# Attention with a conditioning vector: exponentials one by one, the sums of x earlier in VectorE's order, K's halves as Q's, and a rearranged front

## The chip, the core and the metric

The kernel runs on one core of a Trainium2 chip. The core has five engines with instruction queues of their own: TensorE (PE in the profile; its weight loads are shown as PEld), VectorE (DVE), ScalarE (ACT), GpSimd (POOL) and SyncE (SP, which here only issues DMAs). They work side by side and wait for one another through semaphores; each engine works through its own queue in order. Matrix products land in PSUM, which the kernel uses as eight banks of 128 x 512 float32 values; everything else lies in SBUF.

The metric is the device time of one execution in microseconds (us), lower is better. The kernel before takes 751.83 us (median of 3 runs, 751.81 to 753.56).

## The reference

The input `x` is 8 sequences of 512 rows of 512 features, `cond_1024` one vector of 512 for each sequence. All is float32. Cut to what matters:

```python
def reference(x, cond_1024, Wq, bq, Wk, bk, Wv, bv):      # 16 heads of 32
    tokens = cond_1024[:, None, :]
    Q = split_heads(x @ Wq.T + bq)
    K = split_heads(x @ Wk.T + bk)
    V = split_heads(x @ Wv.T + bv)
    cQ = Q + split_heads(tokens @ Wq.T + bq)
    cK = K + split_heads(tokens @ Wk.T + bk)
    scores = einsum('bhqd,bhkd->bhqk', cQ, cK) / sqrt(32)
    out = einsum('bhqk,bhkd->bhqd', softmax(scores), V)
    return x + merge_heads(out)
```

## The kernel before

**Units of work.** Four heads (128 features) of one sequence make one unit t; there are 8 x 4 = 32 of them, and b, r = divmod(t, 4) are its sequence and its group of heads. For each t the scores are computed twice: once with the queries in the rows (`row_scores`, L490), for the row maximum (`row_max_of`, L499, on VectorE, two banks at a time) and for the denominators (`denominators`, L527, four activations on ScalarE that only leave their sums), and once with the keys in the rows (`exponentials`, L569 and L572), where L569 first puts the negative maximum into the bank and L572 adds the scores. ScalarE takes the exponentials out of these banks (L584, L586). They stay in SBUF, and an iteration later `weighted` multiplies them with V (`times_v`, L591).

**The loop.** An iteration t of the main loop (t = 0 to 28) has four steps. Each step opens with `exponentials(t, k)` and `row_max(t+1, ...)`, and then holds one more piece of work on TensorE:

- step 0: a part of the projection Q of the next sequence (`project_pair("q")`);
- step 1: `weighted(t-1)`, and for r = 0 and 1 a half of `combine_x(b+1)`;
- step 2: a part of K's projection;
- step 3: a part of V's projection, and the transposing of the next maxima (`transpose_max`, L553).

At t = 0 the steps hold what is left of the first sequence's projections instead.

**The projections** of all but the first heads are done with seven half-size products in place of eight, per 2 x 2 blocks. `combine_x` makes the sums and differences of blocks of x that this takes (tile `xc`; L321, L322 for half 0, L324, L325 for half 1; each 128 x 512), `combine_w` those of the weights. `first_products` does products 1, 6, the half kc = 0 of product 2, and 7; `other_products` does 4, 5, the rest of product 2, and 3. In steps, Q's and K's first products run at odd r and their other products at even r, V's the other way round: the step for Q and K is one iteration behind (`qk_of`). K differs from Q in how product 2 is divided: in `first_products` only the first 128 of its 256 columns, in `other_products` the second part of these and both parts of the remaining 128 columns, as six matmuls of 128 columns (two per part, each float32 matmul being two instructions in the trace). A copy on GpSimd (L438) stands for the part that the first half leaves out.

**`weighted`** (t-1, in step 1) multiplies on TensorE into one bank, takes the reciprocal of the denominators (L637, VectorE), turns the bank in 32 x 32 blocks into SBUF (L639, VectorE), and leaves the multiplication and the addition of x to GpSimd (L640, L641) before four DMAs write the output.

**Order.** The instruction order on TensorE, ScalarE, VectorE and GpSimd is the program's own, written by hand. PSUM's banks are given out by the table `TURNS`: each step has a row of eight bank numbers; `banks(0..3)` are for the exponentials and, once these are taken out, for the step's further work; `banks(4..7)` are for the row scores. `advance()` goes to the next row; rows 0 to 7 repeat in the loop, 8 to 12 serve the end, 13 to 17 the first denominators before the loop. `banks(i, 2)` gives two banks as one operand with a stride: banks 3 and 7 make one operand of the first step's maximum in row 17.

**The front.** The four row blocks of the first sequence are loaded through SP's and ScalarE's queues, two each, then the conditioning vectors and two biases through ScalarE's (`cond_sb`, L199 to L201) and the weights through SP's. TensorE transposes x (`transpose_x`, L299), then the conditioning (L718), then the weights (`transpose_w`, L254), and projects Q and K of the first heads (L338). A one-column exponential, `table` (L241), makes ScalarE load its function table; it stands behind all constants in the program, behind all the loads on ScalarE's queue.

Of the kernel before, what the change touches and what calls it, by code (L numbers as in the profile page):

```python
# [9 lines left out]
F32 = mybir.dt.float32  # L10
# [7 lines left out]
def kernel(  # L18
# [38 lines left out]
    nc = tc.nc  # L57
# [46 lines left out]
    ]  # L104
    turn = [0]

    def banks(i, n=1):

        j = TURNS[turn[0]][i]
        if n == 1:  # L110
            return psum[:, j, :]
        k = TURNS[turn[0]][i + 1]
        return psum[:, j : k + 1 : k - j, :]
# [13 lines left out]
    def load_x(n, queue=nc.sync):  # L127

        if n < B * NS:
            xs[n] = xp.tile([P, D], F32, tag="x", name=f"x_{n}")  # L130
            queue.dma_start(xs[n], x[n // NS, n % NS * P : (n % NS + 1) * P, :])
# [62 lines left out]
    load_x(1, nc.scalar)  # L194
    load_x(2)
    load_x(3, nc.scalar)

    cond_sb = const.tile([B + 2, D], F32, tag="cond", name="cond_sb")
    nc.scalar.dma_start(cond_sb[:B, :], cond)  # L199
# [16 lines left out]

    ident = const.tile([P, P], F32, tag="ident", name="ident")
    make_identity(nc, ident)
    onesb = const.tile([P, P], BF16, tag="onesb", name="onesb")
    nc.vector.memset(onesb, 1.0)  # L220
    ones = const.tile([P, P], F32, tag="ones", name="ones")
    nc.vector.memset(ones, 1.0)
    split = []
    for i in range(2):
        m = const.tile([P, NS, HG, HD], BF16, tag=f"split{i}", name=f"split{i}")
# [11 lines left out]
    nc.vector.memset(condT, 0.0)  # L237
    identb = const.tile([P, P], BF16, tag="identb", name="identb")
    nc.vector.tensor_copy(identb, ident)
    table = const.tile([P, 1], F32, tag="table", name="table")  # L240
    nc.scalar.activation(table, ones[:, :1], AF.Exp)  # L241
    xc = const.tile([P, 4, 2, HS], F32, tag="xc", name="xc")
    vs = [const.tile([P, NS, D], F32, tag=f"v{i}", name=f"v{i}") for i in range(2)]

# [46 lines left out]
    def transpose_x(n, pt, leaves=nc.vector.tensor_copy):  # L291

        b, sc = divmod(n, NS)
        if b >= B:
            return
        if sc == 0:
            xT[b] = xtp.tile([P, NC, S], F32, tag="xT", name=f"xT_{b}")
        for cc in range(NC):
            nc.tensor.transpose(  # L299
                pt[:, cc * P : (cc + 1) * P], xs[n][:, cc * P : (cc + 1) * P], ident  # L300
            )
        leaves(xT[b][:, :, sc * P : (sc + 1) * P], pt.rearrange("p (c s) -> p c s", c=NC))
        load_block(n + NC)
# [74 lines left out]
    def block_of_x(b, i, kc, at):  # L378
        f = MADE_OF[i - 1][1]
        if isinstance(f, int):  # L380
            return xc[:, f, kc, at]
        off = HS * (f == "22")
        return xT[b][:, kc + 2 * (f != "11"), at.start + off : at.stop + off]

    def product(n, b, u, i, pt, kcs=(0, 1), cols=None):


        for kc in kcs:
            w = block_of_w(n, i, u, kc)
            if n == "v":  # L390
                xb = block_of_x(b, i, kc, slice(u * P, (u + 1) * P))
                nc.tensor.matmul(pt, xb, w, start=(kc == kcs[0]), stop=(kc == kcs[-1]))  # L392
            else:
                xb = block_of_x(b, i, kc, cols or slice(0, HS))
                nc.tensor.matmul(pt, w, xb, start=(kc == kcs[0]), stop=(kc == kcs[-1]))  # L395

    def twice(a):
# [22 lines left out]
    def first_products(n, b, u, dens, small, at, first=0):  # L420

        one_, two_ = banks(first), banks(at)
        c1, c12, c2, c22 = parts_of(n, b, u)
        m1 = c2[:, 0, :]
        product(n, b, u, 1, one_[:, :HS])
        nc.scalar.copy(m1, one_[:, :HS])
        dens()
        product(n, b, u, 6, two_[:, :HS])  # L430
        small()
        w = P if n == "k" else HS
        product(n, b, u, 2, two_[:, HS : HS + w], (0,), slice(0, w))
        product(n, b, u, 7, one_[:, HS:])
        nc.vector.tensor_tensor(c12, two_[:, :HS], m1, ALU.add)
        nc.vector.tensor_tensor(c1[:, 0, :w], two_[:, HS : HS + w], m1[:, :w], ALU.add)
        if w < HS:
            nc.gpsimd.tensor_copy(c1[:, 0, w:], m1[:, w:])  # L438
        plus(n, b, u, 1, c22, one_[:, HS:], c12)

    def other_products(n, b, u, dens, small, at):

        dens()
        one_, two_ = banks(at[0]), banks(at[1])
        product(n, b, u, 4, one_[:, :HS])
        product(n, b, u, 5, one_[:, HS:])
        small()
        if n == "k":
            product(n, b, u, 2, two_[:, :P], (1,), slice(0, P))
            product(n, b, u, 2, two_[:, P:HS], (1, 0), slice(P, HS))  # L450
        else:
            product(n, b, u, 2, two_[:, :HS], (1,))
        product(n, b, u, 3, two_[:, HS:])
        c1, c12, c2, c22 = parts_of(n, b, u)
        nc.vector.tensor_tensor(c12, one_[:, HS:], c12, ALU.add)
        nc.vector.tensor_tensor(c2, halves(one_), twice(c22), ALU.add)
        plus(n, b, u, 0, c1, halves(two_), c1)
        if n != "v":
            for g in range(2):
                qkT[n, b * G + u * 2 + g] = pair_of(b * G + u * 2, n)[:, g, :]  # L460
# [103 lines left out]
    def exponentials(t, kc, at=None):  # L564

        bank = [psum[:, i, :] for i in at] if at else [banks(i) for i in range(HG)]
        for j in range(HG):
            r = slice(j * HD, j * HD + 3)
            nc.tensor.matmul(bank[j], onesb[r, :], maxT[t][r, :], start=True, stop=False)  # L569
        for j in range(HG):  # L570
            r = slice(j * HD, (j + 1) * HD)
            nc.tensor.matmul(  # L572
                bank[j],
                qkT["k", t][r, kc * P : (kc + 1) * P],
                qkT["q", t][r, :],
                start=False,
                stop=True,
            )
        for pr in range(NP):
            e = ep.tile([P, 2, S], F32, tag="e", name=f"e_{t}_{kc}_{pr}")  # L580
            es[t, kc, pr] = e
            if pr == 0 or at:
                for i in range(2):
                    nc.scalar.activation(e[:, i, :], bank[pr * 2 + i], AF.Exp)  # L584
            else:
                nc.scalar.activation(e, banks(2, 2), AF.Exp)  # L586

    def times_v(t, kc, pt, chunks=range(NS)):
        b, g = divmod(t, G)
# [22 lines left out]
        oT[t] = op.tile([P, S], F32, tag="oT", name=f"oT_{t}")  # L612
        nc.vector.tensor_copy(oT[t], pt)

    def weighted(t, pt, pd):


        apart = op.tile([P, HG, NS, NS], F32, tag="apart", name=f"apart_{t}")
        nc.gpsimd.tensor_tensor(
            apart,  # L620
            sums[t].rearrange("p c h o -> p h c o").broadcast_to([P, HG, NS, NS]),
            which.unsqueeze(1).unsqueeze(1).broadcast_to([P, HG, NS, NS]),
            ALU.mult,
        )
        for kc in range(NS):
            times_v(t, kc, pt)
            if kc == 0:
                for h in range(HG):
                    nc.tensor.matmul(
                        pd[h * BL : (h + 1) * BL, : NB],  # L630
                        modulo,
                        apart[:, h].rearrange("p c a -> p (c a)"),
                        start=True,
                        stop=True,
                    )
        rec = op.tile([P, NB, 1], F32, tag="recs", name=f"recs_{t}")
        nc.vector.reciprocal(rec, pd[:, :NB].unsqueeze(2))  # L637
        y = op.tile([P, NB, BL], F32, tag="res", name=f"res_{t}")
        nc.vector.transpose(y.rearrange("p f e -> p (f e)"), pt)  # L639
        nc.gpsimd.tensor_tensor(y, y, rec.broadcast_to([P, NB, BL]), ALU.mult)  # L640
        nc.gpsimd.tensor_tensor(y, y, xr.pop(t), ALU.add)  # L641
        b, g = divmod(t, G)
        for h in range(HG):
            nc.sync.dma_start(spread(out[b], g * P + h * BL), y[h * BL : (h + 1) * BL])
# [67 lines left out]

    for c in range(NS):
        transpose_x(c, bank((3, 7, 0, 1)[c]), nc.scalar.copy if c % 2 else nc.vector.tensor_copy)
    pc = bank(5)
    BB = B + 2
    for cc in range(NC):
# [5 lines left out]
    bias2 = const.tile([P, 2, NC], F32, tag="bias2", name="bias2")  # L723
    nc.vector.tensor_scalar(bias2[:, 0, :], pcv[:, :, B], 2.0 * SCALE, None, ALU.mult)
    nc.vector.tensor_scalar(bias2[:, 1, :], pcv[:, :, B + 1], 2.0, None, ALU.mult)
    for half in range(2):
        combine_x(0, half, nc.gpsimd)
    transpose_w("q", 0, bank(6), 1)
    transpose_w("k", 0, bank(3), 0)
    transpose_w("q", 1, bank(7), 1)  # L730
    pq, pk = bank(4), bank(2)
    for cc in range(NC):
        project_qk_part(0, "q", cc, pq)
# [36 lines left out]
    advance()  # L770
    row_max(0, 3)
    split_max(0)
    first_products("v", 0, 0, lambda: denominators(0, 3), nothing, 2, 0)
    turn_x(NC)
    advance()
    row_max(1, 0)
    transpose_max(0, banks(3), nc.scalar.copy)
    other_products("v", 0, 0, lambda: denominators(1, 0), nothing, (0, 2))
    turn_x(NC + 1)
    load_residual(0)  # L780
# [27 lines left out]
    for t in range(T - 3):  # L808
# [16 lines left out]
        dens = lambda: denominators(t + 1, 2)  # L825
        if t:
            dens()
            weighted(t - 1, banks(0), banks(1))
        else:
            first_products("v", 0, 1, dens, nothing, 1)  # L830
        if r < 2:
            combine_x(b + 1, r)
        advance()

        exponentials(t, 2)
# [166 lines left out]
```

## Time and profile before

| | us |
|---|---|
| median of the runs | 751.83 |
| the profiled execution, its own time | 751.59 |
| its span, from first to last instruction | 749.8 |
| granted TensorE clock, mean | 1.000 |
| TensorE busy (matmuls) | 736.8 (98%) |
| ScalarE busy | 621.6 (83%) |
| VectorE busy | 529.4 (71%) |
| GpSimd busy | 178.6 (24%) |

| group | count | mean ns |
|---|---|---|
| L527 denominators, 128 x 512, ScalarE | 496 | 686 |
| L527 reading their sums | 496 | 204 |
| L584 exponentials, 128 x 512, ScalarE | 270 | 596 |
| L586 exponentials, 128 x 1024, ScalarE | 121 | 1032 |
| L428 copy of the first product, 128 x 256, ScalarE | 46 | 372 |
| L499 row maximum of two banks, VectorE | 256 | 1218 |
| L639 turning of the output, VectorE | 28 | 717 |
| L321, L324 first sum of a half, VectorE | 7, 7 | 654, 650 |
| L322, L325 second sum of a half, VectorE | 7, 7 | 1318, 1536 |
| L640, L641 multiply and add, GpSimd | 28, 28 | 1212, 1425 |
| L395 K's 128-column matmuls of product 2 | 120 | 274 |
| L241 table load, ScalarE | 1 | 1283 |

How to read it: matmuls are pipelined, so that the busy time of TensorE includes overlaps and small waits; 98% doesn't mean that it runs at its peak. The mean of an instruction is the time from its start to its end, and on ScalarE and VectorE the next one can start before that end. What one more instruction costs is read from the distance between starts, and only where the engine is not waiting. What a wait costs is read from the step in which it lies: the starts of the L569 matmuls mark the steps, and the main loop's iterations repeat them very evenly.

### The profile page before, as it was taken

The page shows a single profiled execution, that of the slowest core. Times are in us where ns is not written, and L with a number is a line of the kernel's source. Part 1 is how long each engine was busy: PE and PEld are TensorE (multiplying, and loading weights), DVE is VectorE, ACT ScalarE, POOL GpSimd, SP SyncE. Part 2 cuts the span into 40 slices and gives each one's busy share as a digit, 9 for nine tenths or more (in the row PEclk, how much of TensorE's full clock was granted, in tenths as well). Part 3 has the DMA queues.
Part 4 walks back from the last instruction along what each step waited for, and adds up shares of the span by engine and source line. Part 5 has one row for each costly group of instructions (what it writes and reads, how often), then busy time and mean ns, then how long its engine had stood idle before and what let it go on. Part 6 is the DMA issues. An engine that isn't in the chain of part 4 may idle for free.

```text
span 749.8 us, 14920 instructions
## 1 busy us (share of the span) xinstructions
PE 736.8 (98%) x5494; PEld 411.7 (55%) x5494; DVE 529.4 (71%) x727; ACT 621.6 (83%) x1446; POOL 178.6 (24%) x285
## 2 busy tenths in 40 slices
PE   9999999999999999999999999999999999999897
PEld 6566555655555655555565555555555565555332
DVE  3578777777677776687766876767767777657664
ACT  2459889888898888988888888988889888888965
POOL 3721211223211232211222221122321123221120
PEclk9999999999999999999999999999999999999999
DMA  7502112122212222212222211212110111110111
GB/s 260 81 16 43 29 30 43 30 43 43 37 24 41 36 36 44 44 22 36 39 34 43 43 27 31 44 30 43 29 20 10 29 29 29 29 30 8 29 36 29
DMA packets 184764, 29.63 MB, mean 40 GB/s; under 512 B 178410, under 2 KB 182506, under 8 KB 184692
## 3 DMA queue, kind: packets, MB, share of 16 engines
q1 hardware_dynamic: 184112, 28.01, 21.7%
q8 instruction: 43, 0.70, 0.4%
q10 hardware_dynamic: 580, 0.68, 0.3%
q14 instruction: 29, 0.24, 0.1%
HBM read 20.27 MB, written 8.39 MB: 38 GB/s over the span
## 4 chain that ended last, share of the span: by engine, by line
PE 84%; DVE 7%; ACT 5%; issue 2%; DMA 1%; ACTq 0%; DVEq 0%
PE psum L395 20%; PE psum L591 15%; PE psum L490 14%; PE psum L392 14%; PE psum L572 12%; PE psum L569 5%; ACT dead L527 4%; DVE nmax L499 2%; PE psum L338 2%; DVE xc L325 1%; DVE res L639 1%; DVE xc L322 1%; PE psum L553 1%; PE psum L254 1%; DVE xc L324 1%
## 5 line engine op out<-in xcount | busy, mean ns | idle before, releaser
L499 DVE TENSOR_REDUCE nmax<-psum 128x2 f32<-128x1024 f32 x256 | 301.6, 1218 | 143.8 <-PE psum L490 143.6
L527 ACT ACTIVATE dead<-psum,nmax 128x512 f32<-128x512 f32 x496 | 334.1, 686 | 35.3 <-DVE nmax L499 35.1
L584 ACT ACTIVATE e<-psum 128x512 f32<-128x512 f32 x270 | 145.8, 596 | 59.7 <-PE psum L572 59.3
L490 PE MATMUL psum<-kT,qT 32*128 32x512 f32 x1024 | 141.0, 605 | 1.6 <-ACT e L586 0.3
L640 POOL TENSOR_TENSOR res<-res,recs 128x512 f32<-128x512 f32 x28 | 33.9, 1212 | 435.3 <-DVE res L639 435.3
L572 PE MATMUL psum<-qT,kT 32*128 32x512 f32 x1024 | 134.6, 589 | 0.0
L586 ACT ACTIVATE e<-psum 128x1024 f32<-128x1024 f32 x121 | 124.9, 1032 | 0.0
L591 PE MATMUL psum<-e,v 128*32 128x512 f32 x1024 | 120.3, 596 | 1.0 <-ACT e L586 0.8
L527 ACT ACTIVATION_READ_ACCUMULATOR dead<-psum,nmax 128x1 f32 x496 | 101.4, 204 | 0.0
L490 PEld LDWEIGHTS psum<-kT,qT 32*128 32x128 f32 x1024 | 58.8, 183 | 64.5 <-ACT dead L527 33.2
L591 PEld LDWEIGHTS psum<-e,v 128*32 128x32 f32 x1024 | 26.9, 110 | 65.8 <-issue 41.1
L569 PE MATMUL psum<-maxT,onesb 3*128 3x512 bf16 x512 | 54.6, 384 | 2.8 <-ACT dead L527 1.2
L572 PEld LDWEIGHTS psum<-qT,kT 32*128 32x128 f32 x1024 | 51.3, 185 | 2.3 <-issue 0.2
L569 PEld LDWEIGHTS <-onesb 3*128 3x128 bf16 x512 | 14.4, 91 | 63.8 <-issue 54.2
L392 PE MATMUL psum<-wc_v,xc 128*128 128x256 f32 x192 | 49.3, 379 | 0.0
L395 PE MATMUL psum<-xc,wc_k 128*128 128x256 f32 x180 | 46.2, 379 | 0.0
L395 PE MATMUL psum<-xc,wc_q 128*128 128x256 f32 x180 | 46.2, 379 | 0.0
L639 DVE STREAM_TRANSPOSE res<-psum 128x512 f32<-128x512 f32 x28 | 20.1, 717 | 34.4 <-PE psum L591 18.0
L641 POOL TENSOR_TENSOR res<-res,xr 128x512 f32<-128x512 f32 x28 | 39.9, 1425 | 2.2
L392 PEld LDWEIGHTS psum<-wc_v,xc 128*128 128x128 f32 x192 | 36.5, 190 | 5.0
L392 PE MATMUL psum<-wT_v,xT 128*128 128x256 f32 x128 | 38.7, 404 | 0.0
L395 PEld LDWEIGHTS psum<-xc,wc_q 128*128 128x128 f32 x180 | 34.2, 190 | 4.6
(159 smaller groups left out, 806.2 us busy)
## 6 DMA issues: line engine op xcount, KB each, us to landing
x<-in_x_dram SPq DMA_DIRECT2D x112, 64.0 KB, 2.4
xr<-in_x_dram SPq DMA_DIRECT2D x112, 64.0 KB, 2.5
out_dram<-res SPq DMA_DIRECT2D x112, 64.0 KB, 2.0
w_q<-in_L_cond_Wq_dram SPq DMA_DIRECT2D x4, 256.0 KB, 3.4
w_k<-in_L_cond_Wk_dram SPq DMA_DIRECT2D x4, 256.0 KB, 5.0
w_v<-in_L_cond_Wv_dram SPq DMA_DIRECT2D x4, 256.0 KB, 5.7
xr<-in_x_dram SPq DMA_DIRECT2D x4, 256.0 KB, 3.0
out_dram<-res SPq DMA_DIRECT2D x3, 256.0 KB, 2.3
```

The source lines that it names most:

```text
L392: nc.tensor.matmul(pt, xb, w, start=(kc == kcs[0]), stop=(kc == kcs[-1]))
L395: nc.tensor.matmul(pt, w, xb, start=(kc == kcs[0]), stop=(kc == kcs[-1]))
L490: nc.tensor.matmul(pt, qkT["q", t][r, qc * P : (qc + 1) * P], qkT["k", t][r, :], start=True, stop=True,)
L499: nc.vector.tensor_reduce(nmax[t][:, qc, pr * 2 : pr * 2 + 2, 0], pt, AX.X, ALU.max, negate=True)
L527: nc.scalar.activation(dead, banks(HG + j), AF.Exp, bias=nmax[t][:, qc, j, :], accum_out=sums[t][:, qc, j, :],)
L569: nc.tensor.matmul(bank[j], onesb[r, :], maxT[t][r, :], start=True, stop=False)
L572: nc.tensor.matmul(bank[j], qkT["k", t][r, kc * P : (kc + 1) * P], qkT["q", t][r, :], start=False, stop=True,)
L584: nc.scalar.activation(e[:, i, :], bank[pr * 2 + i], AF.Exp)
L586: nc.scalar.activation(e, banks(2, 2), AF.Exp)
L591: nc.tensor.matmul(pt[j * HD : (j + 1) * HD, :], vs[b % 2][:, kc, (g * HG + j) * HD : (g * HG + j + 1) * HD], es[t, kc, j // 2][:, j % 2, ...
L640: nc.gpsimd.tensor_tensor(y, y, rec.broadcast_to([P, NB, BL]), ALU.mult)
L641: nc.gpsimd.tensor_tensor(y, y, xr.pop(t), ALU.add)
```

## The change

There are five parts.

1. `exponentials`: the third and fourth exponentials are taken out by two activations of 128 x 512 instead of one of 128 x 1024, as the first two are.
2. `weighted` gets a function `between`, which it calls behind the reciprocal and ahead of the turning. Through it the sums of x (`combine_x`, for r = 0 and 1) stand ahead of the turning on VectorE, and no longer behind it. At t = 0 there is no `weighted`, and the sums stay where they were.
3. K's product 2 is divided as Q's: 256 columns of kc = 0 in the first products, 256 columns of kc = 1 in the other ones. The copy on GpSimd goes, and the sum L436 on VectorE has 256 columns for K also.
4. At the front the table load stands behind ScalarE's two loads of x and ahead of the three small loads on the same queue; the two constants of ones are set first. TensorE transposes three blocks of weights ahead of the conditioning, and GpSimd's sums of x and the copies out of these banks move with them in the program's order.
5. In the steps before the loop other banks are used: row 17 of `TURNS`, the second bank of V's first products, and the bank in which the first maxima are transposed.

```diff
-        (4, 2, 5, 6, 3, 7, 0, 1),
+        (4, 7, 5, 6, 2, 3, 0, 1),
...
     load_x(3, nc.scalar)
+    onesb = const.tile([P, P], BF16, tag="onesb", name="onesb")
+    nc.vector.memset(onesb, 1.0)
+    ones = const.tile([P, P], F32, tag="ones", name="ones")
+    nc.vector.memset(ones, 1.0)
+    table = const.tile([P, 1], F32, tag="table", name="table")
+    nc.scalar.activation(table, ones[:, :1], AF.Exp)
...
     def first_products(n, b, u, dens, small, at, first=0):
...
-        w = P if n == "k" else HS
-        product(n, b, u, 2, two_[:, HS : HS + w], (0,), slice(0, w))
+        product(n, b, u, 2, two_[:, HS:], (0,))
         product(n, b, u, 7, one_[:, HS:])
         nc.vector.tensor_tensor(c12, two_[:, :HS], m1, ALU.add)
-        nc.vector.tensor_tensor(c1[:, 0, :w], two_[:, HS : HS + w], m1[:, :w], ALU.add)
-        if w < HS:
-            nc.gpsimd.tensor_copy(c1[:, 0, w:], m1[:, w:])
+        nc.vector.tensor_tensor(c1[:, 0, :], two_[:, HS:], m1, ALU.add)
...
     def other_products(n, b, u, dens, small, at):
...
-        if n == "k":
-            product(n, b, u, 2, two_[:, :P], (1,), slice(0, P))
-            product(n, b, u, 2, two_[:, P:HS], (1, 0), slice(P, HS))
-        else:
-            product(n, b, u, 2, two_[:, :HS], (1,))
+        product(n, b, u, 2, two_[:, :HS], (1,))
...
-            if pr == 0 or at:
-                for i in range(2):
-                    nc.scalar.activation(e[:, i, :], bank[pr * 2 + i], AF.Exp)
-            else:
-                nc.scalar.activation(e, banks(2, 2), AF.Exp)
+            for i in range(2):
+                nc.scalar.activation(e[:, i, :], bank[pr * 2 + i], AF.Exp)
...
-    def weighted(t, pt, pd):
+    def weighted(t, pt, pd, between):
...
         nc.vector.reciprocal(rec, pd[:, :NB].unsqueeze(2))
+        between()
         y = op.tile([P, NB, BL], F32, tag="res", name=f"res_{t}")
         nc.vector.transpose(y.rearrange("p f e -> p (f e)"), pt)
...
+    for half in range(2):
+        combine_x(0, half, nc.gpsimd)
+    transpose_w("q", 0, bank(6), 1)
+    transpose_w("k", 0, bank(3), 0)
+    transpose_w("q", 1, bank(7), 1)
     pc = bank(5)
...
-    for half in range(2):
-        combine_x(0, half, nc.gpsimd)
-    transpose_w("q", 0, bank(6), 1)
-    transpose_w("k", 0, bank(3), 0)
-    transpose_w("q", 1, bank(7), 1)
...
-    first_products("v", 0, 0, lambda: denominators(0, 3), nothing, 2, 0)
+    first_products("v", 0, 0, lambda: denominators(0, 3), nothing, 2, 3)
...
-    transpose_max(0, banks(3), nc.scalar.copy)
+    transpose_max(0, banks(1), nc.scalar.copy)
...
-            weighted(t - 1, banks(0), banks(1))
+            weighted(
+                t - 1, banks(0), banks(1), lambda: combine_x(b + 1, r) if r < 2 else None
+            )
         else:
             first_products("v", 0, 1, dens, nothing, 1)
-        if r < 2:
-            combine_x(b + 1, r)
+            combine_x(1, 0)
```

More of the change, by code (lines that the diff above doesn't have):

```diff
@@ L218 @@
     make_identity(nc, ident)
[L219 to L222, printed above, removed]
     split = []
@@ L239 @@
     nc.vector.tensor_copy(identb, ident)
-    table = const.tile([P, 1], F32, tag="table", name="table")
-    nc.scalar.activation(table, ones[:, :1], AF.Exp)
     xc = const.tile([P, 4, 2, HS], F32, tag="xc", name="xc")
@@ L383, in block_of_x, with product @@
         return xT[b][:, kc + 2 * (f != "11"), at.start + off : at.stop + off]
-    def product(n, b, u, i, pt, kcs=(0, 1), cols=None):
+    def product(n, b, u, i, pt, kcs=(0, 1)):
         for kc in kcs:
@@ L393, in product @@
             else:
-                xb = block_of_x(b, i, kc, cols or slice(0, HS))
+                xb = block_of_x(b, i, kc, slice(0, HS))
                 nc.tensor.matmul(pt, w, xb, start=(kc == kcs[0]), stop=(kc == kcs[-1]))
```

## The prediction

> **What bounds the kernel now.** I read three views: the page's chain of waits, the timeline around one iteration, and the timelines of single engines. The chain says which engine sets the time:
>
> ```profile
> PE 84%; DVE 7%; ACT 5%; issue 2%; DMA 1%; ACTq 0%; DVEq 0%
> ```
>
> TensorE is the bound, and some 13% of the chain is time in which it waits for VectorE and ScalarE. To place that, I took from the timeline the starts of the L569 matmuls, one group of which opens each step (four steps per t, r = t mod 4). They repeat to 0.01 us: r=0: 5.26, 5.77, 5.50, 6.01 = 22.54; r=1: 5.26, 5.75, 5.06, 6.46 = 22.53; r=2: 5.26, 5.77, 5.50, 5.63 = 22.16; r=3: 5.26, 5.75, 5.06, 5.86 = 21.93. Step 3 does the same matmuls for every r, yet takes 5.63 to 6.46. VectorE's timeline at t=8 (r=0, first five rows) and at t=10 (r=2, last three) shows why:
>
> ```profile
> 240.99 0.25 DVE L637 RECIPROCAL recs<-psum 128x16 f32<-128x16 f32 x1
> 242.49 0.72 DVE L639 STREAM_TRANSPOSE res<-psum 128x512 f32<-128x512 f32 x1 [1.26 <-issue]
> 243.13 0.65 DVE L321 TENSOR_TENSOR xc<-xT 128x512 f32<-128x512 f32 x1
> 243.82 1.42 DVE L322 TENSOR_TENSOR xc<-xc,xT 128x512 f32<-128x512 f32 x1
> 245.16 2.34 DVE L499 TENSOR_REDUCE nmax<-psum 128x2 f32<-128x1024 f32 x2
> ...
> 286.06 0.25 DVE L637 RECIPROCAL recs<-psum 128x16 f32<-128x16 f32 x1
> 287.57 0.72 DVE L639 STREAM_TRANSPOSE res<-psum 128x512 f32<-128x512 f32 x1 [1.26 <-issue]
> 289.56 1.23 DVE L499 TENSOR_REDUCE nmax<-psum 128x2 f32<-128x1024 f32 x1 [1.27 <-PE psum L490]
> ```
>
> VectorE stands idle 1.26 us before the turning L639, waiting for TensorE, then does the two sums of x (L321/L322, at r=1 L324/L325), and the row maximum of step 2 starts late: 2.67 us after the turning began, against 1.99 at r=2. ScalarE's denominators start late in turn, their banks come free late, and TensorE pays in step 3. In the sequence at the front two more waits carry weight, for the conditioning's DMA and at the first transposing of the maxima:
>
> ```profile
> 7.51 0.41 PE L718 MATMUL psum<-ident,cond_sb 10*128 10x10 f32 x4 [0.52 <-DMA cond_sb<-in_L_cond_bk_dram]
> ...
> 50.38 0.38 PE L553 MATMUL psum<-identb,split 128*128 128x128 bf16 x4 [1.47 <-DVE nmax L499]
> ```
>
> **The change, part by part.** All sums are against the profiled execution: 751.59 us, span 749.8, 1.8 outside it. The median of the runs is 0.24 above it.
>
> 1. *Sums of x ahead of the turning* (r=0 and 1). The reciprocal ends at 241.24. One sum took 0.65; the other, which takes 1.42 to 1.54 here, ran in 0.69 at t=0, where GpSimd was idle (L640/L641 run beside it in all other rows). In the new place GpSimd is idle too: L640 waits for the turning, after 15.4 us of nothing. Two sums: 0.65 + 0.69 = 1.34 less some 0.07 of overlap, so VectorE is free at about 242.5, when TensorE releases the turning anyway (242.49). What hides the sums is that wait of 1.26 us (1.20 at r=1). The turning's bank is wanted by the row scores of step 2 at 243.39 (bank 7, second matmul); L639 would end at 243.2 to 243.3, just in time. So r=0 and r=1 become like r=2 and r=3: 22.54 - 22.16 = 0.38 and 22.53 - 21.93 = 0.60.
>
> 2. *K's halves as Q's.* The columns are the same (128 + 128 + 2x128 before, 2x256 after). But six matmuls of 128 columns go at 0.11 us each (0.66 from 246.18 to 246.84) where two pairs of 256 would give 0.43: step 2 of even r falls from 5.50 to Q's 5.27, that of odd r, with two more half-width passes, rises from 5.06 to 5.27. At even r the 0.23 is kept: step 3 there is released by K's last sum (L418), which follows TensorE's own last product and moves with it. At odd r the 0.21 is given back by step 3: its row scores at 315.86 waited 0.2 for the last denominator (ended 315.81), which runs from ScalarE's first exponential and doesn't move; 5.86 becomes 5.63. VectorE's L436 grows from 0.28 to 0.42, GpSimd's 0.29 copy goes; both beside TensorE.
>  After 1 and 2: even r 5.26 + 5.77 + 5.27 + 5.63 = 21.93; odd r 5.26 + 5.75 + 5.27 + 5.63 = 21.91. Gains: r=0 0.61 x 6 (t=4 to 24), r=1 0.62 x 7, r=2 0.23 x 7, r=3 0.02 x 7, and 0.23 each at t=0 and t=28, where K's second half stands: 3.7 + 4.3 + 1.6 + 0.1 + 0.5 = 10.2.
>
> 3. *Exponentials singly* (121 pairs). ScalarE's timeline, a pair and what follows it, then four singles of the tail:
>
> ```profile
> 300.76 1.03 ACT L586 ACTIVATE e<-psum 128x1024 f32<-128x1024 f32 x1
> 301.72 0.37 ACT L428 COPY qT<-psum 128x256 f32<-128x256 f32 x1
> ...
> 723.89 2.06 ACT L584 ACTIVATE e<-psum 128x512 f32<-128x512 f32 x4 [1.42 <-PE psum L572]
> ```
>
>  A pair holds the engine 0.96 us (300.76 to 301.72). Singles start 0.48 to 0.49 apart, so two hold it as long. But their ends come 0.49 apart: four end after 2.06, while two and a pair end after 2.00 (at 255.09 two took 1.08, the pair began at 256.06 and took 1.03). So between 0 and 0.06 us per pair. The Trainium skill speaks against the change: "ScalarE: Activation LUTs", section "What ACT_TABLE_LOAD costs", gives an activation 186 ns plus 0.833 ns per column, with 93 ns of overlap between neighbours, so that a second instruction adds 93 ns. Who pays: in most steps the denominators wait 0.16 to 0.22 for the row maximum, which absorbs it. In the steps of a "first" product a copy (L428) fills that gap and the last denominator ends only 0.07 before the row scores that reuse its bank: V at even r, Q and K at odd r, 42 steps. By the rows 0 to 2.6 us, by the skill's rule an estimated 42 x 0.093 = 3.9; I take 0.03 a step, 1.3, the rows' middle. What the singles free earlier, the third bank, nobody waits for outside the tail (0.3 before L490 on the page).
>
> 4. *Front: sums and weights ahead of the conditioning; table load early.* TensorE's x transposes end at 6.99, it then waits for the vectors until 7.51. The first chunks of Wq and Wk are there by 6.4, the second of Wq by 7.5. Three weight blocks at 0.44 from 6.8, then the four small transposes (0.34): Q's projection starts near 8.45 instead of 9.38, its weights' copy ending near 8.25. Gain 0.9. The table load (1.28) now stands between ScalarE's second load of x (issued by 1.64) and the three small loads, so the first two of these go out near 3.2 and 3.8 instead of 1.66 and 2.28. The third, the last to land, was not issued before 4.50 and still isn't; it is wanted at 8.1 and lands at 7.46. Queued behind it on ScalarE: only the x copies. SP's queue is untouched. GpSimd's four sums still wait for the last x copy (7.61).
>
> 5. *Other banks.* The L553 transposes had their data at 48.84 (their weights load began) and yet waited until 50.38, for a row maximum that reads banks 3 and 7 as one strided pair: bank 6, theirs, lies between. With pairs (2,3) and (0,1) and bank 7 as target, the wait is for V's last sum there (48.30). Gain 1.5. What is late next: the denominators of t=1, which end about 0.1 before they are wanted. Against it, K's first half here adds 0.2.
>
>  Sum: 10.2 + 0.9 + 1.5 - 0.2 - 1.3 = 11.1. 751.59 - 11.1 = 740.5; with the median's 0.24, 740.7.
>
> **The rivals.** *Singles at the skill's price:* 3.9 instead of 1.3, 743.3; for it, the 0.07 of slack; against it, starts 0.48 apart. *The move brings nothing:* if the turning, late by the sums, holds bank 7 about as long as the row maximum was late, items 4, 5 and K's r=2 remain: 0.9 + 1.5 - 0.2 + 1.6 + 0.6 - 1.3 = 3.1, 748.7. For it: only 0.1 between L639's end and its bank's next use; against: the idle 1.26. *More than forecast:* step 3 loses its last waits (0.07 x 28), singles cost nothing: 737.4. *Slower:* the sums take 1.42 to 1.54 each in their new place, 2.9 together from 241.17. The turning then ends 1.5 after the time at which bank 7 is wanted (it has until 1.4), TensorE stands still in step 2 of 13 iterations, 19.5 us against some 11: 760. It decides from sums of 2.3 us. Against it: nothing of GpSimd's runs there. That the exponentials' bank pairs or the small loads' later issue do nothing at all is inside the first case.
>
> **How the numbers follow.** Forecast 0.66; singles at the skill's price 0.12; more than forecast 0.10; move brings nothing 0.07; slower 0.05. The range runs from 737 (no waits left in step 3, free singles) to 744.5 (the skill's price and half of the front's gain lost). A run of this kernel can tell 0.3% (2.3 us) from no change. Faster takes every case but the last, less a little for a mixture that ends near nothing: 0.92; same 0.03; slower 0.05.
>
> **What would show it.** Right: L639 still starts 1.5 us after L637, L322 and L325 take 0.7, step 2's maximum starts 1.1 after its L490, and all four r take 21.9. The front: projection at 8.5, L553 without its 1.47, t=0 starting at about 51.6 instead of 53.77. Wrong: L490 of step 2 waiting for L639; step lengths after first products growing by more than 0.06; the small loads landing after 8.1.

## The result, and the profile after

The changed kernel takes **741.18 us** (median of 5 runs, 741.04 to 741.48), the kernel before 752.08 beside it (5 runs, 751.81 to 753.56). The ratio is 0.985, 95% interval 0.9836 to 0.9864: about 10.9 us less. The forecast was 740.7. The profiled execution took 741.09, its span is 739.3 (before 749.8), the granted clock 0.999.

From the page of the changed kernel, the chain of waits and two of the costliest groups (busy us, mean ns, idle before):

```profile
PE 97%; ACT 1%; DMA 1%; DVE 1%; issue 0%; SPq 0%; DVEq 0%; ACTq 0%
...
L630 POOL TENSOR_TENSOR res<-res,recs 128x512 f32<-128x512 f32 x28 | 29.4, 1049 | 438.5 <-DVE res L629 438.5
...
L631 POOL TENSOR_TENSOR res<-res,xr 128x512 f32<-128x512 f32 x28 | 35.7, 1274 | 2.2
```

In this chain VectorE's and ScalarE's shares have gone from 7% and 5% to 1% each. The prediction took its 13% for time in which TensorE waits. It can't all be that: the two shares fell by 10% of the span, some 75 us, while the span fell by 10.5. The span less TensorE's busy time was 13.0 us (749.8 - 736.8) and is 8.9 (739.3 - 730.4); the other 6.4 came off its busy time, which includes small waits. The prediction's sum doesn't suffer from it, since it is made from step lengths.

The lines are numbered anew: the turning is L629 (was L639), the reciprocal L626, the row maximum L490, the row scores L481, the L569 that opens a step is L560. GpSimd's two operations, which had run beside the sums of x, fell from 1212 and 1425 ns to 1049 and 1274. The view of groups by shape gives the other side of it, the second sums on VectorE, first before, then after:

```profile
L322 DVE TENSOR_TENSOR xc<-xc,xT 128x512 f32<-128x512 f32 x7 | 9.2, 1318 | 0.2
L325 DVE TENSOR_TENSOR xc<-xT,xc 128x512 f32<-128x512 f32 x7 | 10.8, 1536 | 0.0
...
L322 DVE TENSOR_TENSOR xc<-xc,xT 128x512 f32<-128x512 f32 x7 | 4.8, 692 | 0.2
L325 DVE TENSOR_TENSOR xc<-xT,xc 128x512 f32<-128x512 f32 x7 | 4.7, 678 | 0.0
```

VectorE's timeline at t=8 shows the new order:

```profile
237.02 0.25 DVE L626 RECIPROCAL recs<-psum 128x16 f32<-128x16 f32 x1
237.19 0.63 DVE L321 TENSOR_TENSOR xc<-xT 128x512 f32<-128x512 f32 x1
237.85 0.69 DVE L322 TENSOR_TENSOR xc<-xc,xT 128x512 f32<-128x512 f32 x1
238.53 0.72 DVE L629 STREAM_TRANSPOSE res<-psum 128x512 f32<-128x512 f32 x1
240.52 2.36 DVE L490 TENSOR_REDUCE nmax<-psum 128x2 f32<-128x1024 f32 x2 [1.27 <-PE psum L481]
```

The idle 1.26 before the turning is gone; the sums lie in its place. The turning still starts 1.51 after the reciprocal, and the maximum of step 2 comes 1.99 after the turning, as it did at r=2 before. From the starts of the L560 matmuls, in us per step (usual iterations; three are longer after the change, see the end):

| | before | after |
|---|---|---|
| r=0 | 5.26, 5.77, 5.50, 6.01 = 22.54 | 5.26, 5.77, 5.26, 5.63 = 21.93 |
| r=1 | 5.26, 5.75, 5.06, 6.46 = 22.53 | 5.26, 5.77, 5.26, 5.65 = 21.95 |
| r=2 | 5.26, 5.77, 5.50, 5.63 = 22.16 | 5.26, 5.77, 5.26, 5.63 = 21.93 |
| r=3 | 5.26, 5.75, 5.06, 5.86 = 21.93 | 5.26, 5.77, 5.26, 5.65 = 21.95 |
| t=0 begins at | 53.77 | 52.23 |

The front, in TensorE's timeline (start, us from the first to the last of the group), one row of before and then the rows after:

```profile
9.38 1.10 PE L338 MATMUL psum<-xT,wT_q 128*128 128x512 f32 x2
```

```profile
6.63 0.60 PE L254 MATMUL psum<-ident,w_q 128*128 128x128 f32 x4
7.50 0.63 PE L254 MATMUL psum<-ident,w_k 128*128 128x128 f32 x4 [0.27 <-DMA w_k<-in_L_cond_Wk_dram]
8.17 0.63 PE L254 MATMUL psum<-ident,w_q 128*128 128x128 f32 x4
8.80 0.38 PE L713 MATMUL psum<-ident,cond_sb 10*128 10x10 f32 x4
9.11 0.70 PE L338 MATMUL psum<-xT,wT_q 128*128 128x512 f32 x1
...
48.82 0.40 PE L544 MATMUL psum<-identb,split 128*128 128x128 bf16 x4
```

The 0.52 for the conditioning is gone, but Q's projection starts only 0.27 earlier (9.11 against 9.38): TensorE now waits for the weights. The first transposing of the maxima (L544, was L553) has lost its wait of 1.47.

### The profile page after: what moved, and what is told of

Read it like the earlier page. It is cut to its first block, busy times and chain, and to the rows that moved or that the text cites. A ratio compares the mean times of both kernels' runs of the same rounds, so it can differ in the third digit from the quotient of the medians.

```text
span 739.3 us, 14941 instructions
## 1 busy us (share of the span) xinstructions
PE 730.4 (99%) x5434; PEld 407.5 (55%) x5434; DVE 523.4 (71%) x727; ACT 629.4 (85%) x1567; POOL 166.6 (23%) x270
## 4 chain that ended last, share of the span: by engine, by line
PE 97%; ACT 1%; DMA 1%; DVE 1%; issue 0%; SPq 0%; DVEq 0%; ACTq 0%
PE psum L394 26%; PE psum L481 16%; PE psum L579 16%; PE psum L563 15%; PE psum L391 14%; PE psum L560 6%; PE psum L338 2%; PE psum L544 1%; DMA w_k<-in_L_cond_Wk_dram 1%; ACT e L574 1%; PE psum L254 1%; PE psum L638 0%; PE psum L589 0%; PE psum L677 0%; PE psum L618 0%
## 5 line engine op out<-in xcount | busy, mean ns | idle before, releaser
L490 DVE TENSOR_REDUCE nmax<-psum 128x2 f32<-128x1024 f32 x256 | 301.8, 1220 | 158.1 <-PE psum L481 156.6
L574 ACT ACTIVATE e<-psum 128x512 f32<-128x512 f32 x512 | 264.3, 602 | 59.6 <-PE psum L563 59.4
L481 PE MATMUL psum<-kT,qT 32*128 32x512 f32 x1024 | 142.0, 605 | 0.1
L563 PE MATMUL psum<-qT,kT 32*128 32x512 f32 x1024 | 132.4, 588 | 0.0
L630 POOL TENSOR_TENSOR res<-res,recs 128x512 f32<-128x512 f32 x28 | 29.4, 1049 | 438.5 <-DVE res L629 438.5
L481 PEld LDWEIGHTS psum<-kT,qT 32*128 32x128 f32 x1024 | 58.7, 183 | 60.7 <-ACT dead L518 29.9
L560 PE MATMUL psum<-maxT,onesb 3*128 3x512 bf16 x512 | 51.3, 384 | 1.6 <-DVE maxT L550 0.9
L560 PEld LDWEIGHTS <-onesb 3*128 3x128 bf16 x512 | 13.3, 91 | 60.4 <-issue 51.0
L394 PEld LDWEIGHTS psum<-xc,wc_k 128*128 128x128 f32 x180 | 34.2, 190 | 4.6
L631 POOL TENSOR_TENSOR res<-res,xr 128x512 f32<-128x512 f32 x28 | 35.7, 1274 | 2.2
L170 POOL TENSOR_TENSOR xr<-xr,bvs 128x512 f32<-128x512 f32 x28 | 35.6, 1271 | 0.2 <-issue 0.2
(157 smaller groups left out, 739.2 us busy)
```

What stands on the lines that cost most here:

```text
L170: nc.gpsimd.tensor_tensor(xr[t], xr[t], bias, ALU.add)
L481: nc.tensor.matmul(pt, qkT["q", t][r, qc * P : (qc + 1) * P], qkT["k", t][r, :], start=True, stop=True,)
L490: nc.vector.tensor_reduce(nmax[t][:, qc, pr * 2 : pr * 2 + 2, 0], pt, AX.X, ALU.max, negate=True)
L563: nc.tensor.matmul(bank[j], qkT["k", t][r, kc * P : (kc + 1) * P], qkT["q", t][r, :], start=False, stop=True,)
```

## The experiments

Theory: the sums, at 0.65 and 0.69, hide in the wait ahead of the turning, and this gives most of the gain; K's halves, the banks and the front give the rest, the singles cost little. Rivals: the singles cost more or help; the gain belongs to another part; the sums are short for a reason other than an idle GpSimd. Medians of 4 to 9 runs each. Kernels with one part put back (sums, K's halves, banks, pairs) ran on one chip, where the changed kernel was not run; they are compared with its 741.18, and the kernel before took 752.2 there. The others say what ran beside them. A time holds 1.7 to 3.0 us outside the span, and this part scatters too; where a few tenths matter, the spans on record for each run are given.

**The changed kernel again.** It gives the scatter from chip to chip.

> The changed kernel itself, to stand beside the others on this chip: 741.0 to 741.5; iterations 21.93 at even r and 21.95 at odd r; the projection of the first heads starts at 9.1, within 0.3, by when the weights land.

Measured: 741.22 (741.05 to 741.42), ratio 0.9852 (0.9837 to 0.9867). The same. Spans: 739.2 to 739.5, against 739.3 to 739.5 the first time.

**The sums back behind the turning.**

```diff
-            weighted(
-                t - 1, banks(0), banks(1), lambda: combine_x(b + 1, r) if r < 2 else None
-            )
+            weighted(t - 1, banks(0), banks(1), nothing)
+            if r < 2:
+                combine_x(b + 1, r)
```

> The changed kernel with the sums of x behind the turning again. Theory (GpSimd's multiplication and addition run beside the sums, the second takes 1.4 to 1.5 us, the row maximum of step 2 starts 0.65 late): r=0 back to about 22.54, r=1 to 22.53, so 6 x 0.61 + 7 x 0.58 = 7.7 us more, 748.9. Rival (the late turning costs what the early maximum gains): 741.2.

Measured: 749.54 (749.27 to 752.53), ratio 0.9973 (0.9961 to 0.9984). 8.4 us of the gain are given back by this part alone. In VectorE's timeline of this kernel the idle time and the long second sum are both there again:

```profile
241.89 0.72 DVE L629 STREAM_TRANSPOSE res<-psum 128x512 f32<-128x512 f32 x1 [1.26 <-issue]
242.53 0.65 DVE L321 TENSOR_TENSOR xc<-xT 128x512 f32<-128x512 f32 x1
243.21 1.42 DVE L322 TENSOR_TENSOR xc<-xc,xT 128x512 f32<-128x512 f32 x1
244.56 1.21 DVE L490 TENSOR_REDUCE nmax<-psum 128x2 f32<-128x1024 f32 x1
```

and the loss stands in step 3 alone: 6.25 for 5.63 at r=0, 6.31 for 5.65 at r=1; r=2 and r=3 don't change. Over the 13 iterations that is 8.3 us. (The profiled execution took 752.47; what it has beyond the median lies ahead of the loop, which begins at 53.70 instead of 52.23, and in one step of t=29, 7.41 for 5.86.)

**The move alone, in the kernel before.**

```diff
         nc.vector.reciprocal(rec, pd[:, :NB].unsqueeze(2))
+        between()
...
-            weighted(t - 1, banks(0), banks(1))
+            weighted(
+                t - 1, banks(0), banks(1), lambda: combine_x(b + 1, r) if r < 2 else None
+            )
...
-        if r < 2:
-            combine_x(b + 1, r)
+            combine_x(1, 0)
```

> The kernel before with only one part of the change: the two sums of x placed between the reciprocal and the turning; everything else, K's halves too, stays old. Theory (the two sums at 0.65 + 0.69 fit into the wait of 1.26 us before the turning): r=0 goes from 22.54 to K-old's 22.16, r=1 from 22.53 to 21.93, so 6 x 0.38 + 7 x 0.60 = 6.5 us, 745.5 us; the t=0 iteration starts where it did before (53.8). Rival (the gains of the move and of K's halves need each other, so that each alone gives little): 750 or more.

Measured: 745.58 (745.47 to 745.64), before on that chip 752.12, ratio 0.9915 (0.99 to 0.9929): 6.5 less. r=0 takes 22.17, r=1 21.93. So the move stands on its own. It is worth 6.5 with K's old halves and 8.4 with the new ones. With the sums behind the turning K's new halves give nothing at r = 0 and 1 (22.55 and 22.61 in the kernel above, 22.54 and 22.53 before): what step 2 gains there, step 3 loses.

**K's old halves in the changed kernel.**

```diff
-        product(n, b, u, 2, two_[:, HS:], (0,))
+        w = P if n == "k" else HS
+        product(n, b, u, 2, two_[:, HS : HS + w], (0,), slice(0, w))
...
-        product(n, b, u, 2, two_[:, :HS], (1,))
+        if n == "k":
+            product(n, b, u, 2, two_[:, :P], (1,), slice(0, P))
+            product(n, b, u, 2, two_[:, P:HS], (1, 0), slice(P, HS))
+        else:
+            product(n, b, u, 2, two_[:, :HS], (1,))
```

> The changed kernel with K's product 2 divided as before. Theory: step 2 of even r and at t=0 and t=28 is 0.23 longer (15 x 0.23 = 3.45), odd r unchanged in sum (5.06 + 5.86 for 5.27 + 5.65), the front 0.2 shorter: 3.2 us more, 744.4. Rival (even and odd cancel): 741.2.

Measured: 743.93 (743.88 to 745.34), ratio 0.9894 (0.9881 to 0.9906): 2.75 more than the changed kernel. Even r goes to 22.17 (step 2 5.50); odd r stays at 21.95, with 5.06 and 5.86 for 5.26 and 5.65. K's halves gain where the prediction put it, and what odd r loses in step 2 comes back in step 3. By the steps they are worth 3.5; the changed kernel gives 0.7 of it back in three longer iterations (t=11, 22 and 26, see the end), which this kernel doesn't have.

**The old banks in the first step.**

```diff
-        (4, 7, 5, 6, 2, 3, 0, 1),
+        (4, 2, 5, 6, 3, 7, 0, 1),
...
-    first_products("v", 0, 0, lambda: denominators(0, 3), nothing, 2, 3)
+    first_products("v", 0, 0, lambda: denominators(0, 3), nothing, 2, 0)
...
-    transpose_max(0, banks(1), nc.scalar.copy)
+    transpose_max(0, banks(3), nc.scalar.copy)
```

> The changed kernel with the old banks in the steps ahead of the loop. Theory (the first maxima's transposes wait for a row maximum whose two banks, 3 and 7, enclose theirs): 1.5 us more, 742.7, and the 1.47 us wait is back. Rival (the wait goes with the earlier front): 741.2, no such wait.

Measured: 742.48 (742.22 to 743.78), ratio 0.9873 (0.9861 to 0.9886): 1.3 more, 0.9 in the profiles' spans (740.2 against 739.3). The loop begins 1.64 later, at 53.87, and the three longer iterations are gone, which gives 0.7 back. The wait is back, in TensorE's timeline of this kernel:

```profile
50.48 0.38 PE L544 MATMUL psum<-identb,split 128*128 128x128 bf16 x4 [1.38 <-DVE nmax L490]
```

The bank numbers are the only edit, and the wait ends with the first row maximum, which reads banks 3 and 7 and not bank 6, into which the transposing writes. So the wait comes from the choice of banks, and by these numbers from the strided pair that encloses bank 6. The pair and the target were changed together, neither alone.

**Something beside the sums.** Two multiplications on GpSimd, computed in addition and used by nothing, are started by the reciprocal, at r = 0 and 1:

```diff
         between()
+        if t % G in (G - 1, 0):
+            for _ in range(2):
+                load = op.tile([P, NB, BL], BF16, tag="load", name=f"load_{t}_{_}", bufs=1)
+                nc.gpsimd.tensor_tensor(
+                    load, xr[t], rec.broadcast_to([P, NB, BL]), ALU.mult
+                )
```

> The changed kernel with two more multiplications of 128 x 512 on GpSimd in 14 of the iterations (r = 0 and 1), started by the reciprocal, their results unused. Theory (a VectorE sum of two SBUF operands is slowed by such an operation on GpSimd): the sums take 0.65 and 1.4 or more instead of 0.63 and 0.69, the turning starts 0.7 later and ends at or past the time at which its bank is wanted, step 2 or 3 of these iterations grows by 0.3 to 0.8, 4 to 10 us in all. Rival (the second sum was slow in its old place for another reason, the row maximum or the turning before it): sums unchanged, turning unchanged, at most 1 us more from the later output.

Measured: 749.28 (748.87 to 751.39), ratio 0.9966 (0.9956 to 0.9977): 8.1 more than the changed kernel (741.22 on that chip). First VectorE's, then GpSimd's, then TensorE's timeline at t=8 (L635 is the turning here, L631 the added multiplications):

```profile
238.97 0.25 DVE L626 RECIPROCAL recs<-psum 128x16 f32<-128x16 f32 x1
239.13 0.63 DVE L321 TENSOR_TENSOR xc<-xT 128x512 f32<-128x512 f32 x1
239.79 1.42 DVE L322 TENSOR_TENSOR xc<-xc,xT 128x512 f32<-128x512 f32 x1
241.13 0.70 DVE L635 STREAM_TRANSPOSE res<-psum 128x512 f32<-128x512 f32 x1
```

```profile
239.29 2.82 POOL L631 TENSOR_TENSOR load<-xr,recs 128x512 bf16<-128x512 f32 x2 [13.69 <-DVE recs L626]
```

```profile
241.37 1.65 PE L481 MATMUL psum<-kT,qT 32*128 32x512 f32 x8
```

The same row scores in the changed kernel:

```profile
239.43 1.02 PE L481 MATMUL psum<-kT,qT 32*128 32x512 f32 x8
```

With GpSimd at work the second sum takes 1.42 in the new place too (1.53 at r=1). The turning starts 2.16 after the reciprocal instead of 1.51, and the row scores of step 2, eight instructions, take 1.65 instead of 1.02: the turning ends at 241.83, and they wait for its bank. Step 2 grows from 5.26 to 5.89 at r=0 and to 5.86 at r=1. So it is the idle GpSimd that makes the sums short, and there is next to no slack behind them: 0.65 on VectorE costs 0.62 on TensorE. Moved, but beside GpSimd, the sums cost nearly as much as unmoved (749.28 against 749.54), though in step 2 and no longer in step 3.

**Exponentials of the third and fourth bank in pairs again.**

```diff
-            for i in range(2):
-                nc.scalar.activation(e[:, i, :], bank[pr * 2 + i], AF.Exp)
+            if pr == 0 or at:
+                for i in range(2):
+                    nc.scalar.activation(e[:, i, :], bank[pr * 2 + i], AF.Exp)
+            else:
+                nc.scalar.activation(e, banks(2, 2), AF.Exp)
```

> The changed kernel with the third and fourth exponentials as one activation of 1024 columns again. Theory (singles end 0.06 us later and delay TensorE only where a step follows a 'first' product): steps 1 and 3 of odd r fall from 5.77 and 5.65 by 0.02 each, 0.5 to 1.3 us in all, 739.9 to 740.7. Rival (each single costs 0.093 us more, 42 steps): 737.3. Rival (singles help, because banks come free sooner): slower than 741.2.

(The 0.093 us of the first rival is the skill's 93 ns, which the prediction quotes.) Measured: 741.95 (741.04 to 742.29), ratio 0.9861 (0.9848 to 0.9874). Taken alone this would say that singles help by 0.7. The spans and the steps say otherwise. The spans are 739.2, 739.2, 739.3 and 740.5, where the changed kernel has 739.3 to 739.5; two of the four executions spent 2.7 us outside their span, where the changed kernel's spent 1.7 to 2.1. In the loop, step 1 of odd r takes 5.75 for 5.77 and step 3 of t=28 5.19 for 5.26; step 3 of t=14 takes 5.71 for 5.63, and nothing else changes by more than 0.01. ScalarE's timelines of a usual step, first with the pair, then with singles:

```profile
255.97 1.08 ACT L575 ACTIVATE e<-psum 128x512 f32<-128x512 f32 x2 [0.27 <-PE psum L563]
256.94 1.03 ACT L577 ACTIVATE e<-psum 128x1024 f32<-128x1024 f32 x1
258.16 0.69 ACT L518 ACTIVATE dead<-psum,nmax 128x512 f32<-128x512 f32 x1 [0.19 <-DVE nmax L490]
```

```profile
255.78 2.06 ACT L574 ACTIVATE e<-psum 128x512 f32<-128x512 f32 x4 [0.25 <-PE psum L563]
257.98 0.69 ACT L518 ACTIVATE dead<-psum,nmax 128x512 f32<-128x512 f32 x1
```

The last exponential ends 2.00 after the first began with the pair (257.97) and 2.06 with singles (257.84). But from the first exponential to the first denominator it is 2.19 and 2.20, since the row maximum ends last in both (258.06 and 257.88).

**The table load at its old place,** the weights still first; run on two chips.

```diff
-    table = const.tile([P, 1], F32, tag="table", name="table")
-    nc.scalar.activation(table, ones[:, :1], AF.Exp)
...
+    table = const.tile([P, 1], F32, tag="table", name="table")
+    nc.scalar.activation(table, ones[:, :1], AF.Exp)
     xc = const.tile([P, 4, 2, HS], F32, tag="xc", name="xc")
```

> The changed kernel with the table load at its old place behind all constants, the weights still ahead of the conditioning. Theory (with the table load early the second and third small load go out at 4.40 and 5.68 instead of 2.28 and 4.50 and land at 8.7, the second chunk of Wq lands at 8.0 instead of 7.8; TensorE waits for both): projection of the first heads at 8.65 instead of 9.11, 0.4 us less than the changed kernel. Rival (the early table load frees ScalarE for the copies of x and is worth its place): 0.2 us more. Rival (it makes no difference): the same within 0.2.

> The changed kernel with the table load at its old place, a second time, beside the two that follow. Theory (the early table load costs some 0.4 us): 740.8 us. Rival (the 0.44 us of the first time were scatter): 741.2.

Measured: 740.78 (740.7 to 741.15; the changed kernel on that chip 741.22), and 741.6 (741.34 to 742.98) on another chip, where the changed kernel was not run. The first alone would have confirmed the 0.4 in its times (spans 738.9 to 739.3 against 739.2 to 739.5); the second doesn't. The sign that the theory gave, Q's projection at 8.65, didn't come: it starts at 9.25 and 9.18, in the changed kernel at 9.11 and 9.25. So no gain is shown, and the profiles don't place one. What ScalarE's queue did is plain, first in the changed kernel, then with the late load (second run; L207 and L205 are the third small load):

```profile
1.66 1.28 ACT L202 ACT_TABLE_LOAD   x1 [1.66 <-PEq L979]
1.73 0.54 ACTq L205 DMA_DIRECT2D cond_sb<-in_cond_dram  x1
...
4.40 0.23 ACTq L206 DMA_DIRECT2D cond_sb<-in_L_cond_bq_dram  x1
5.68 0.23 ACTq L207 DMA_DIRECT2D cond_sb<-in_L_cond_bk_dram  x1
```

```profile
1.67 0.58 ACTq L203 DMA_DIRECT2D cond_sb<-in_cond_dram  x1
2.28 0.23 ACTq L204 DMA_DIRECT2D cond_sb<-in_L_cond_bq_dram  x1
4.88 0.23 ACTq L205 DMA_DIRECT2D cond_sb<-in_L_cond_bk_dram  x1
```

The early table load didn't hold back the first small load (1.73, while the load runs until 2.94), but it changed when the others went out: the second went out 2.1 later, the third 0.8 later. In the changed kernel each of these two is issued when a load of x has landed, on whose semaphore it waits. SP's queue changed as well: Wq's second block was issued at 2.60 instead of 4.70. As long as three blocks of weights stand ahead, TensorE hardly waits for the small loads any more: its four small transposes follow the weights' at once, at 8.80, and after 0.15 in the second profile of the changed kernel.

**The conditioning ahead of the weights again,** the table load early.

```diff
-    for half in range(2):
-        combine_x(0, half, nc.gpsimd)
-    transpose_w("q", 0, bank(6), 1)
-    transpose_w("k", 0, bank(3), 0)
-    transpose_w("q", 1, bank(7), 1)
     pc = bank(5)
...
+    for half in range(2):
+        combine_x(0, half, nc.gpsimd)
+    transpose_w("q", 0, bank(6), 1)
+    transpose_w("k", 0, bank(3), 0)
+    transpose_w("q", 1, bank(7), 1)
     pq, pk = bank(4), bank(2)
```

> The changed kernel with the conditioning's transposes ahead of the weights again, the table load early. Theory (the last small load lands at 8.7): TensorE waits for it until 8.8, projection at 10.6, 1.5 us more than the changed kernel. Rival (the small loads land as before, at 7.5): projection at 9.4, 0.3 more.

Measured: 742.48 (742.07 to 742.73), ratio 0.9868 (0.9853 to 0.9883): 1.26 more than the changed kernel on the same chip. TensorE's timeline of this kernel:

```profile
8.45 0.39 PE L708 MATMUL psum<-ident,cond_sb 10*128 10x10 f32 x4 [0.92 <-DMA cond_sb<-in_L_cond_bq_dram]
...
10.30 1.10 PE L338 MATMUL psum<-xT,wT_q 128*128 128x512 f32 x2
```

The wait of 0.52 has become 0.92. With the late table load and the same order, in the kernel before, Q's projection started at 9.38 and 9.81, here at 10.30. The early table load is harmless only behind the other edit of the front.

**Two attempts at a faster kernel,** both with the late table load, on the chip of its second run: pairs again, and the conditioning between the first blocks of Wq and Wk (`transpose_w("k", 0, ...)` and `transpose_w("q", 1, ...)` moved behind the four small transposes).

> The changed kernel with the table load at its old place and the exponentials of the third and fourth bank in pairs as before. Theory A (singles cost 0.02 us in step 1 of odd r and nothing else, 0.3 us in all): 740.5 us, 0.3 below the one with singles. Theory B (pairs hold the third bank longer and cost something): 741.2 or more. Theory C (no difference): 740.8.

> The changed kernel with the table load at its old place and, in the front, the conditioning's four small transposes between the first block of Wq and that of Wk, where TensorE waits some 0.3 us for Wk. Theory (the three small loads land at about 7.5 when the table load stands behind them): the 0.34 us of the transposes lie in the wait for Wk, Q's projection starts 0.2 to 0.4 earlier, 740.5 us. Rival (the third small load lands after 7.8, or VectorE's small copies push the second Wq block's copy back): 741 or more.

Measured: 741.19 (740.92 to 741.89) and 741.1 (741.05 to 742.82), beside 741.6 for the late table load alone. With pairs all four r take 21.92 to 21.93, where singles have 21.95 at odd r; the span is 739.1 against 739.4. In the other kernel the third small load released TensorE at 7.89, the conditioning took the place of the wait for Wk, and Q's projection started at 9.16 against 9.18: the rival, no gain. Neither beats the change by more than the chips differ. Run times don't settle the singles' sign: the first kernel with pairs came out 0.7 above singles on another chip, this one 0.4 below them on the same chip. The spans agree with the steps in sign both times (here 738.9 to 739.2 with pairs, 739.2 to 739.6 and once 740.8 with singles): the singles cost 14 x 0.02 and 0.06 once, some 0.3 us.

## Why the prediction was right, point by point

The sum was 11.1 us; the spans differ by 10.5, the medians by 10.9. Its terms, from the step lengths:

| term | predicted | measured |
|---|---|---|
| sums moved, K's halves (part 1, 2) | 10.2 | 9.9 (with pairs, from the step lengths) |
| singles (part 3) | -1.3 | -0.3 |
| front (part 4) | 0.9 | 0.27 |
| first banks, K's first half there | 1.5 - 0.2 | 1.27 (1.54 at t=0's start, less the front) |
| three longer iterations | none | -0.7 |

- *The move* was right in its mechanism and place: the sums take what they took beside an idle GpSimd, the turning starts 1.51 after the reciprocal, and r=0 and r=1 became like r=2 and r=3. The Trainium skill, page "SBUF — State Buffer", section "SBUF: two separate sides", says that a VectorE instruction with two SBUF inputs and a GpSimd instruction that reads SBUF exclude each other, and that the one which starts first holds the port. The rows of the kernel with the added multiplications agree: a first sum that starts 0.16 before GpSimd's multiplication takes 0.63 beside it, the second, which starts after it, takes 1.42 instead of 0.69.
- *K's halves*: even r as computed to 0.01 us; odd r 21.93 with pairs, against the 21.91 of the sum.
- *The rival "slower"* was right in its mechanism and in its limit; it didn't come true because nothing of GpSimd's runs there. It gave the two sums until 1.4 us. With GpSimd at work they take 2.1 together, and 13 iterations lose 0.60 to 0.63 each, where its line gives 2.1 - 1.4 = 0.7. So there is next to no slack beyond the 1.23 to 1.36 that they take now, and part 1's "just in time" holds. Its 760 is for both sums slow, 2.9 together, which was not run; with one slow the time was 749.3, by its line 741.2 + 13 x 0.7 = 750.3.
- *Singles*: the step that missed is "a copy (L428) fills that gap and the last denominator ends only 0.07 before the row scores". Of the 42 steps that were counted at 0.03, only the 14 that follow Q's copy (step 1 of odd r) pay, 0.02 each; 28 pay nothing that the profile shows. Four singles do end 0.06 later than two and a pair, the upper end of what the prediction read from its rows; the skill's 93 ns, which gave 3.9, is not reached.
- *The front* is the mis-sized term, 0.9 for 0.27. "The first chunks of Wq and Wk are there by 6.4, the second of Wq by 7.5" was too early: TensorE is released by the semaphore of the whole load. In the profile before, Wk's first block landed 5.0 after its issue at 2.12, so at 7.1, and Wq's second 3.4 after 4.31, at 7.8. After the change they landed at 7.36 and 8.04, and TensorE took them at 7.50 and 8.17. The small loads "near 3.2 and 3.8" went out at 1.73 and 4.40. And "The third, the last to land, was not issued before 4.50 and still isn't" with its landing at 7.46 was wrong: it went out at 5.68, and "SP's queue is untouched" was wrong too (Wq's second block went out at 2.60 instead of 4.31). It landed at 8.7, so the sign that was to show an error, small loads landing after 8.1, did come. Its lateness cost next to nothing, since the weights were late as well: TensorE was busy with them until 8.80 and then took it without a wait (in the second profile of this kernel it stood still for 0.15). t=0 began at 52.23 instead of 51.6.
- *The first banks* did what the sum says ahead of the loop; that the longer iterations come with them was not foreseen.
- *Not foreseen*: in the profile of the changed kernel three iterations (t=11, 22 and 26) are longer by 0.2 to 0.26, 0.7 in all. They cancel most of what the singles didn't cost.

So the total came close because the large term was right. That it came as close as 0.5 us is luck: the front gave 0.6 less than counted, the move with K's halves 0.3 less, and the longer iterations took 0.7, while the singles cost 1.0 less.

## What to carry to other kernels

An engine that waits has room for work that stands behind the wait in its queue; check that the work's duration there is the one you count on, by looking at who else runs in that window, since two operations that exclude each other are short only when apart. Before making an engine's work shorter, look for a strided operand over several banks: in this program a write to the bank that lay between waited for the reader of the pair. A share in the chain of waits tells which waits are there, not what they cost; step lengths tell that. And a change of a few tenths of a microsecond can't be judged by run times of different chips; spans and step lengths from the profile settle it better.

## What the hardware showed that was not expected

- **Three longer iterations.** Step 0 of t=11 (5.49), step 1 of t=22 (6.02) and step 0 of t=26 (5.54) are longer in every profile of a kernel that has both the new halves of K and the new first banks, at the same places, whether ScalarE takes singles or pairs; in the kernel before, and with the old halves, the old first banks, or the move alone, they are not there. At t=11 VectorE's row maximum starts 0.54 after TensorE's next work began, where it is 0.17 in the same step of t=15, with nothing in the trace that released it late. The cause is left open.
- **The first loads.** TensorE's first transposing of x began at 4.43 to 4.97 us in the profiles, with the same loads ahead of it. The front of the kernel before, seen twice, started Q's projection at 9.38 and at 9.81. So the 0.27 of the two profiles is uncertain by about as much: on the chip where both were profiled together, the old front stood at 9.81 and the new order of weights (with the late table load) at 9.18.
- **A table load and a DMA issue side by side.** ScalarE's queue issued a load at 1.73 while the table load ran from 1.66 to 2.94.
